# A four-layer graph network on one core: storing one running-maximum row per pair of steps, and a node tile's transform in one piece

## The chip, the cores and the metric

The kernel runs on one core of a Trainium2 chip. The metric is device time of one execution in microseconds (us); smaller is better. A core has a matrix engine (PE, with its weight loads shown as PEld), a vector engine (DVE), an activation engine (ACT), a general engine that also builds the descriptors of indirect transfers (POOL), and a queue engine (SP) that here only issues transfers. Every engine works through its own queue strictly in order and waits on semaphores for the others. Transfers run on 16 DMA engines.

## The reference, cut to what matters

6250 nodes of 256 features and 100000 edges, sorted by destination `dst`. `dst` is drawn as 6250 times a squared uniform number, so nodes of small number have many edges: block by block the mean number of edges per node falls from over a hundred to about eight.

```python
deg = segment_sum(ones, dst)
h = relu(layernorm(x))
h = h @ W1_self + (segment_sum(h[src], dst) / max(deg, 1)) @ W1_neigh + b1     # layer 1, mean
hp = relu(h @ W2_pool + b2_pool)
hmax = segment_max(hp[src], dst)                                               # layer 2, max
h = h @ W2_self + hmax @ W2_neigh + b2
h = ((segment_sum(h[src], dst) + h) / (deg + 1)) @ W3_neigh + b3               # layer 3
h = h @ W4_self + (segment_sum(h[src], dst) / max(deg, 1)) @ W4_neigh + b4     # layer 4, mean
out = x + h @ W_fc + b_fc
```

The hidden width is 512. All of it is float32; the kernel carries float32 through the matrix engine's bf16 path by three bf16 parts of a row.

## The kernel before, in words

Nodes lie in 49 tiles of 128. The weights are multiplied together ahead of the work, so that a layer's dense part is one product per tile. `fast_path` holds all that is spoken of here; `general_path` runs afterwards only if a flag in the tile `bad` says that the edges did not fit what the fast path assumes.

**Layer 1** (lines 780 to 866). Neighbour sums of the first 8 tiles (the hubs) are dense products with an edge-count matrix that is built from one-hot matrices (`build`, L309; `dense`, L433). Those of the other 41 tiles come from `sums` (L356): 474 steps, each an indirect gather of 128 edge rows (POOL, L376 `ring<-tab_h`) and three matmuls with a one-hot matrix (L394). When a tile's sums are complete its `done1` runs: the mean, two transposes (L825), a copy to SBUF (L827), a product with `Wb` (L834), then the rows of `hp` are written to `tab_p` (L838). The tile's own rows are handled apart in `own1` (L788): transposed by six matmuls (L794), copied, multiplied by `Wa` (L804), and the result plus a bias row is written to `tab_g`; `done1` reads that row block back (`grow2`, L819) and adds it. Both halves of the transposed rows also go to `tab_t`, which layer 2 reads. `own1` is advanced from inside `sums` by the iterator `beside`, so in program text all of it stands in the first 200 or so of the 474 steps.

**Layer 2** (lines 1008 to 1198). The 782 columns of edges are cut into six blocks of 52, 100, 200, 200, 130 and 100 columns (`BLOCKS`), worked from the last block to the first. Within a block of `tb` columns partition p holds `tb` consecutive edges. A step takes one column: an indirect gather of 128 rows of `tab_p` into half of a tile X (POOL, L1145), and one DVE instruction (L1150), X = max(previous X times `same`, X), in which `same` is 1 where the edge has the destination of the edge before it in the partition. So X is the running maximum of the run of equal destinations. After a pair of steps both rows of X, 512 KB, are stored to `runs[b]` (SP, L1181). There are six such X tiles in rotation. At a block's end `carry` joins runs over partitions (scan along the partitions, gather, maximum, scatter: L1023, L1035, L1041, L1042); its row number is `fixI`, from `segments`. Only then can `done2` of a node tile gather the row of each node's run end (L1054, at the row numbers `rows_of` from `node_rows`), transpose it, multiply (L1078, L1081, L1084), add (L1088), split into three parts and write `tab_r`. Beside this, `early_products` takes node tiles 37 to 6 in batches of four and multiplies them already for layer 3: per batch 16 results of 12 matmuls (L433 `pd<-r,ae`), each added by DVE to an accumulator (L942).

**Layers 3 and 4** have the shape of layer 1's `sums` with dense products for the first 16 and 18 tiles; the change does not touch them.

What sets the order: the Python text interleaves generators by step, but the order in which instructions stand in an engine's queue is made from it by a scheduler that works with its own estimate of each instruction. An instruction added in one place can move others on the same queue.

Of the kernel before, what the change touches and what calls it, by code (L numbers as in the profile page):

```python
# [25 lines left out]
G = 4  # L26
BLOCKS = (52, 100, 200, 200, 130, 100)
Z_SIGMA = 5.0
# [20 lines left out]
@with_exitstack  # L49
def kernel(ctx, tc, *aps):  # L50
    nc = tc.nc
    keep = ctx.enter_context(tc.tile_pool(name="keep", bufs=1))
    bad = keep.tile([P, 8], F32, name="bad")
    nc.vector.memset(bad, 0.0)
    fast_path(tc, bad, *aps)
    with tc.tile_pool(name="fl", bufs=1) as fp, tc.tile_pool(name="flp", bufs=1, space=PSUM) as pp:
        worst = fp.tile([P, 1], F32, name="worst")
        nc.vector.tensor_reduce(worst, bad, AX.X, ALU.max)
        ones = fp.tile([P, P], F32, name="ones_f")
        nc.vector.memset(ones, 1.0)  # L60
        pw = pp.tile([P, 1], F32, name="pw_f")
        nc.tensor.matmul(pw, ones, worst, start=True, stop=True)
        odd = fp.tile([P, 1], F32, name="odd")
        nc.vector.tensor_scalar(odd, pw, 1.0, None, op0=ALU.min)
        oddI = fp.tile([P, 1], I32, name="oddI")
        nc.vector.tensor_copy(oddI, odd)
        general = nc.values_load(oddI[:1, :1], min_val=0, max_val=1)
    with tc.If(general > 0):
        general_path(tc, *aps)
# [3 lines left out]
def fast_path(  # L73
# [82 lines left out]
    tab_p = dram.tile([NP, FH], F32, name="tab_p")  # L156
    tab_g = dram.tile([NP, FH], F32, name="tab_g")
    tab_r = dram.tile([NP, 3 * FH], BF16, name="tab_r")
    tab_s = dram.tile([NP, 3 * FO], BF16, name="tab_s")
    tab_a = dram.tile([H4, P, NT, P // 2], BF16, name="tab_a")  # L160
    xq = dram.tile([NP, FO], F32, name="xq")
    runs = [dram.tile([tb * P + 1, FH], F32, name=f"runb{b}") for b, tb in enumerate(BLOCKS)]
    dflat = dram.tile([EX + 32], I32, name="dflat")
# [5 lines left out]
    with tc.tile_pool(name="pads", bufs=1) as pp:  # L169
# [13 lines left out]
        nc.scalar.dma_start(sflat[E:EX].rearrange("(a b) -> a b", a=32), pads)  # L183
        for b, tb in enumerate(BLOCKS):
            nc.scalar.dma_start(runs[b][tb * P : tb * P + 1, :], zrow)

# [168 lines left out]

    def sums(pool, psg, table, F, srcT, keyT, jb, h, done, deep, hub, wait=0, counts=0, todo=(),  # L356
             beside=iter(())):

# [24 lines left out]
        for g in range(g_of[h][0], NG):  # L383
            pg = bank(psg, "pg", "pg", (F + counts,))
            n = min(G, T - g * G)
            for k in range(n):
# [13 lines left out]
                if at > wait:  # L400
                    hub.advance(math.ceil(len(hub.work) * (at - wait) / (T - j0 - wait)))
                next(beside, None)
                if todo and next(todo[0], None) is None:
# [47 lines left out]
    def scratch(n, dt=F32):  # L451

        t = xpool.tile([P, G2, FH], F32, name="X2").rearrange("p a b -> p (a b)")
        return (t if dt == F32 else t.bitcast(dt))[:, :n]

    def segments():
        dstI, dstF, eqf = scratch(T, I32), scratch(T), scratch(T)
        flen = ahead.tile([P, 1], F32, name="flenf")
        for b, tb in enumerate(BLOCKS):
# [11 lines left out]
        for b, tb in enumerate(BLOCKS):  # L471
# [7 lines left out]
            nc.vector.tensor_reduce(flen, eqf[:, sl_], AX.X, ALU.add)  # L479
            nc.vector.tensor_scalar(flen, flen, -1.0, float(P), op0=ALU.add, op1=ALU.mult)  # L480
            nc.vector.tensor_add(fixI[:, b : b + 1], flen, pidx)
            yield 1

# [293 lines left out]
    with ExitStack() as on:  # L777
# [9 lines left out]

        def own1(d):  # L788

            pt = bank(pst, "pt", "pt_h", (KI, P))  # L790
            for k in range(KI):
                for part in range(3):
                    c = part * FI + k * P
                    nc.tensor.matmul(pt[:, k, :], Z1[:, d, c : c + P], ident_b,  # L794
                                     start=(part == 0), stop=(part == 2))
            hT = wk.tile([P, KI, P], F32, name="h0T")
            nc.scalar.copy(hT, pt)
            nc.sync.dma_start(tab_t[d, :, : KI * P].rearrange("p (k n) -> p k n", n=P), hT)
            yield 1
            yield 1  # L800
            yield 1
            pm = bank(psm, "pm", "pm_g")
            for k in range(KI):
                nc.tensor.matmul(pm, hT[:, k, :], Wa[:, k, :], start=(k == 0),  # L804
                                 stop=(k == KI - 1))
            g = wk.tile([P, FH], F32, name="grow")
            nc.vector.tensor_add(g, pm, crow)
            nc.sync.dma_start(tab_g[d * P : (d + 1) * P, :], g)
            yield 1

        def done1(d, acc):
# [5 lines left out]
            nc.scalar.activation(m1, acc[:, :FI], AF.Copy, scale=r)  # L817
            g = wk.tile([P, FH], F32, name="grow2")
            nc.sync.dma_start(g, tab_g[d * P : (d + 1) * P, :])  # L819
            yield 1  # L820
            yield 1
            yield 1
            pt = bank(pst, "pt", "pt_m", (KI, P))
            for k in range(KI):
                nc.tensor.transpose(pt[:, k, :], m1[:, k * P : (k + 1) * P], ident)  # L825
            th = wk.tile([P, KI, P], F32, name="th")
            nc.scalar.copy(th, pt)  # L827
            nc.sync.dma_start(tab_t[d, :, KI * P :].rearrange("p (k n) -> p k n", n=P), th)
            yield 1
            yield 1  # L830
            yield 1
            ph = bank(psm, "pm", "pm_hp")
            for k in range(KI):
                nc.tensor.matmul(ph, th[:, k, :], Wb[:, k, :], start=(k == 0),  # L834
                                 stop=(k == KI - 1))
            nc.vector.tensor_add(g, ph, g)
            nc.scalar.activation(g, g, AF.Relu)
            nc.sync.dma_start(tab_p[d * P : (d + 1) * P, :], g)  # L838

# [13 lines left out]
        todo.append(segments())  # L853

        def owns():

            hubs = list(range(H1))
            for i, d in enumerate(range(H1, NT)):
                yield from own1(d)
                if i % 3 == 2 and hubs:  # L860
                    yield from own1(hubs.pop(0))
            for d in hubs:
                yield from own1(d)

        sums(wk, psg, tab_h, FI, srcT, keyT, JC * P, H1, done1, 14, hub, counts=1, todo=todo, beside=owns())
    layer1.close()


    def node_rows(pool, psm):
# [27 lines left out]
        for b, tb in enumerate(BLOCKS):  # L897
            z = float(tb * P)
            nc.vector.tensor_scalar(q, end, float(offs[b + 1]), -1.0 - offs[b], op0=ALU.min,
# [12 lines left out]
            nc.vector.tensor_add(pF, pF, off)  # L912
            nc.vector.scalar_tensor_tensor(t_, off, -float(tb), t_, op0=ALU.mult, op1=ALU.add)
            nc.vector.scalar_tensor_tensor(t_, t_, float(P), pF, op0=ALU.mult, op1=ALU.add)
            nc.vector.tensor_scalar(t_, t_, -z, None, op0=ALU.add)
# [31 lines left out]
    with tc.tile_pool(name="fl2c", bufs=1) as ck, ExitStack() as late:  # L947
# [188 lines left out]
        for b in reversed(range(NB)):  # L1136
# [3 lines left out]
            for s0 in range(0, tb, G2):  # L1140
                n = min(G2, tb - s0)
                X = (xmore if at // G2 % 2 else xpool).tile([P, G2, FH], F32, name="X2")
                for k in range(n):
# [34 lines left out]
                    for g in list(now):  # L1178
                        if next(g, 0) == 0:
                            now.remove(g)  # L1180
                nc.sync.dma_start(  # L1181
                    runs[b][s0 * P : (s0 + n) * P, :].rearrange("(g p) f -> p g f", p=P),
                    X[:, :n, :],
# [777 lines left out]
```

## Time and profile before

| what | us |
|---|---|
| runs | 3230.57, 3235.05, 3228.00; median 3230.57 |
| the profiled execution's own time | 3230.57 |
| its span | 3228.8 |
| layer 1, first gather to first gather of layer 2 | 147.75 to 855.0 |
| layer 2, first gather to last DVE step (L1150) | 855.0 to 2174.2 |
| layer 2, from there to the last gather of a run end (L1054) | 2174.2 to 2281.5 |
| layers 3 and 4 | to 3228.8 |

Counted along the gathers of L1145, layer 2's blocks begin at 855.0, 1006.0, 1222.3, 1546.1, 1879.3 and 2056.8 us: 1.51, 1.66, 1.62, 1.67, 1.78 and 2.24 us per step.

In the page's second part the span is cut into 40 slices of 80.7 us and each digit is a busy share in tenths. In a group of instructions the numbers after the bar are total busy time in us and the mean in ns of one, then the idle time of that engine just ahead of them and what ended it. In a list of waits each line gives who waited for whom, total us, times, and the longest. A table of stretches gives busy us and instruction count of each engine, then the granted PE clock, the DMA share and GB/s.

### The profile page before, as it was taken

Reading aid. Unit: us, or ns where it says so; the run is one execution under the profiler, and the core shown is the slowest. Engines: PE = TensorE matmul, PEld = TensorE weight load, DVE = VectorE, ACT = ScalarE, POOL = GpSimd, SP = SyncE. Lnnn points to the kernel's source line nnn. Section 1 sums busy time; section 2 is a strip of 40 time slices with the busy share of each in tenths; the row PEclk is TensorE's granted clock in tenths of the full one; section 3 lists DMA queues with packets and bytes.
Section 4 is the critical chain, followed back from the end, with each engine's and each line's share of the span. In section 5 each row is a group of like instructions: output and inputs, shape, how many; then the busy total and the mean of one; then the engine's idle time right before and its main releaser. Section 6 shows DMA issues by size and latency. Waiting matters only on the chain. (4 is left out here: it accounts for less than half of the span.)

```text
span 3228.8 us, 41603 instructions
## 1 busy us (share of the span) xinstructions
PE 2489.4 (77%) x12699; PEld 1410.8 (44%) x12699; DVE 1965.7 (61%) x5124; ACT 904.1 (28%) x2432; POOL 2032.8 (63%) x2260
## 2 busy tenths in 40 slices
PE   1468999888667566676677677679599999799997
PEld 1233666666433222233233233234234444488876
DVE  4854667665467676556556665553266767667665
ACT  2555667665245666211101110100000001000000
POOL 5272567777566766777666765550377767577764
PEclk9688999999889677888888888789899999899999
DMA  5454787777899999999999999991599999877774
GB/s 182 158 156 161 228 251 242 231 230 243 265 398 370 370 389 343 389 382 387 346 326 374 388 366 326 311 319 44 233 368 396 393 373 382 303 222 218 216 208 146
DMA packets 424577, 939.06 MB, mean 291 GB/s; under 512 B 60416, under 2 KB 166098, under 8 KB 424312
## 3 DMA queue, kind: packets, MB, share of 16 engines
q0 software_dynamic: 146560, 514.74, 47.1%
q1 hardware_dynamic: 219700, 366.14, 30.9%
q10 hardware_dynamic: 58084, 55.44, 5.3%
q8 instruction: 103, 1.69, 0.2%
q14 instruction: 130, 1.06, 0.1%
HBM read 623.50 MB, written 313.39 MB: 290 GB/s over the span
## 5 line engine op out<-in xcount | busy, mean ns | idle before, releaser
L1145 POOL DMA_INDIRECT X<-tab_p,srcIf x782 | 821.9, 1051 | 410.0 <-issue 185.4
L394 PE MATMUL pg<-ring,hot 128*128 128x256 bf16 (+2 forms) x3390 | 680.1, 310 | 114.0 <-DMA ring<-tab_h,srcT 63.7
L376 POOL DMA_INDIRECT ring<-tab_h,srcT x474 | 450.8, 951 | 239.4 <-PE pg L394 97.2
L433 PE MATMUL pd<-zt,ac 128*128 128x256 bf16 (+1 forms) x3462 | 571.4, 300 | 30.9 <-DMA ac<-tab_a 24.5
L433 PE MATMUL pd<-r,ae 128*128 128x512 bf16 x1536 | 407.0, 415 | 217.8 <-DVE acc L942 149.0
L394 PEld LDWEIGHTS <-hot 128*128 128x128 bf16 x3390 | 330.4, 99 | 343.7 <-issue 169.1
L1150 DVE SCALAR_TENSOR_TENSOR X<-X,samef,X 128x512 f32<-128x512 f32 x385 | 289.2, 751 | 278.9 <-DMA X<-tab_p,srcIf 191.4
L376 POOL DMA_INDIRECT ring<-tab_r,srcE x342 | 332.8, 973 | 150.2 <-PE pg L394 59.8
L433 PEld LDWEIGHTS <-ac 128*128 128x128 fp8e4 x3462 | 340.5, 99 | 165.6 <-issue 22.4
L1150 DVE SCALAR_TENSOR_TENSOR X<-X,samef 128x512 f32<-128x512 f32 x391 | 293.0, 750 | 172.5 <-DMA X<-tab_p,srcIf 168.1
L376 POOL DMA_INDIRECT ring<-tab_s,srcE x314 | 297.9, 949 | 129.0 <-PE pg L394 64.9
L433 PEld LDWEIGHTS <-ae 128*128 128x128 fp8e4 x1536 | 161.0, 105 | 473.1 <-issue 345.1
L309 PE MATMUL pb<-hm,hs 128*128 128x392 bf16 x781 | 257.4, 376 | 139.4 <-ACT A L313 63.1
L301 ACT ACTIVATE hs<-ht,onef 128x128 bf16<-128x128 bf16 x781 | 290.6, 395 | 232.0 <-PE pb L309 206.5
L414 DVE SCALAR_TENSOR_TENSOR acc<-pg,M,acc 128x257 f32<-128x257 f32 (+2 forms) x518 | 274.4, 561 | 79.5 <-PE pg L394 78.2
L1084 PE MATMUL pm_prf<-unf,hTf 128*128 128x512 f32 x392 | 203.1, 644 | 26.2 <-ACT hTf L1075 22.7
L1217 DVE TENSOR_SCALAR_CACHE_REDUCE many<-ac 128x896 bf16<-128x896 fp8e4 (+2 forms) x144 | 138.8, 964 | 129.5 <-DMA ac<-tab_a 129.5
L372 DVE TENSOR_SCALAR hot<-iota_bf,keyE 128x128 bf16<-128x128 bf16 x656 | 151.1, 273 | 67.5 <-PE pg L394 60.5
L303 DVE TENSOR_SCALAR hm<-iota_w,mk 128x392 bf16<-128x392 f16 x461 | 153.6, 339 | 60.0 <-PE pb L309 58.5
L313 ACT ACTIVATE A<-pb 128x392 fp8e4<-128x392 f32 x288 | 140.2, 491 | 170.8 <-PE pb L309 121.3
L433 PE MATMUL pd<-Z,A 128*128 128x256 bf16 (+1 forms) x1176 | 186.4, 273 | 0.4
L309 PEld LDWEIGHTS <-hs 128*128 128x128 bf16 x781 | 81.1, 104 | 225.1 <-issue 105.0
(275 smaller groups left out, 2819.1 us busy)
## 6 DMA issues: line engine op xcount, KB each, us to landing
runb<-X SPq DMA_DIRECT2D x391, 512.0 KB
tab_r<-r SPq DMA_DIRECT2D x49, 384.0 KB
tab_a<-A SPq DMA_DIRECT2D x18, 784.0 KB
tab_g<-grow SPq DMA_DIRECT2D x49, 256.0 KB
grow<-tab_g SPq DMA_DIRECT2D x49, 256.0 KB
tab_p<-grow SPq DMA_DIRECT2D x49, 256.0 KB
th<-tab_t ACTq DMA_DIRECT2D x49, 256.0 KB
X<-tab_p,srcIf POOLq DMA_INDIRECT x782
```

Of the source, the lines that this page charges most:

```text
L301: nc.scalar.activation(hots[0], t, AF.Relu, bias=one, scale=-1.0)
L303: nc.vector.tensor_scalar(hots[1], iota_w, mk[:, r : r + 1], None, op0=ALU.is_equal)
L309: nc.tensor.matmul(hold[0], hots[0], hots[1], start=(k == 0), stop=(k == k_of[w] - 1))
L313: nc.scalar.copy(A[:, :, c : c + WIN], hold[0].rearrange("p (s c) -> p s c", c=WIN), saturate=True)
L372: nc.vector.tensor_scalar(hot[j], iota_b, keyT[:, j - jb : j - jb + 1], None, op0=ALU.is_equal)
L376: nc.gpsimd.indirect_dma_start(out=ring[:, j % deep, : 3 * F], out_offset=None, in_=table, in_offset=bass.IndirectOffsetOnAxis(ap=srcT[:, ...
L394: nc.tensor.matmul(pg[:, : F + c], hot[j], X[:, part * F : (part + 1) * F + c], start=(k == 0 and part == 2), stop=(k == n - 1 and part == 1),
L414: nc.vector.scalar_tensor_tensor(acc[d], pg, m, acc[d], op0=ALU.mult, op1=ALU.add)
L433: nc.tensor.matmul(hold[0][:, : F + c], a, z[:, part * F : (part + 1) * F + c], start=(s == ss[0] and part == 2), stop=(s == ss[-1] and pa ...
L1084: nc.tensor.matmul(pm, hT[:, c, :], un[:, c, :], start=False, stop=(c == KH - 1))
L1145: nc.gpsimd.indirect_dma_start(out=X[:, k, :], out_offset=None, in_=tab_p, in_offset=bass.IndirectOffsetOnAxis(ap=srcI[:, t : t + 1], axis=0),
L1150: nc.vector.scalar_tensor_tensor(X[:, k, :], prev, same[:, t : t + 1], X[:, k, :], op0=ALU.mult, op1=ALU.max,)
```

## The change

Layer 2. For blocks 0, 1 and 2 (`MERGED = 3`) a pair of steps stores one row instead of two. After the pair's two steps one more DVE instruction forms, in the tile's first row, max(second row times `same` of the second step, first row): the second row where the second edge goes on with the run of the first, else the first row, which is then a run's end. Only that row, 256 KB, is stored; the last pair of a block still stores both. `runs[b]` has `tb // 2 + 1` row groups in these blocks; row numbers in `segments` and `node_rows` are converted by `kept_row`. A run that lies wholly in the second step of a pair would be lost, so `bad` gets three more columns that flag it. The cut between blocks 2 and 3 moves from 200 and 200 columns to 220 and 180.

Layer 1. `own1`, `owns`, `tab_g` and `beside` go. `done1` does the six own transposes and the two of the mean into one bank, copies them at once, writes them to `tab_t` with one transfer, and accumulates the products with `Wa` and `Wb` in one bank, to which the bias row is added. It has three yields where it had six.

```diff
-BLOCKS = (52, 100, 200, 200, 130, 100)
+BLOCKS = (52, 100, 220, 180, 130, 100)
+MERGED = 3
...
+    kept = [tb // 2 + 1 if b < MERGED else tb for b, tb in enumerate(BLOCKS)]
+    runs = [dram.tile([n * P + 1, FH], F32, name=f"runb{b}") for b, n in enumerate(kept)]
...
-                next(beside, None)
...
+    def kept_row(b, t, whole, half):
+        nc.vector.tensor_copy(whole, t)
+        nc.vector.tensor_single_scalar(whole, whole, 1, op=ALU.logical_shift_right)
+        nc.vector.tensor_copy(half, whole)
+        nc.vector.tensor_scalar(t, t, -(BLOCKS[b] / 2.0 - 1.0), None, op0=ALU.add)
+        nc.vector.tensor_tensor(t, t, half, op=ALU.max)
...
+            if b < MERGED:
+                two = eqf[:, t0 : t0 + tb // 2 - 1]
+                nc.vector.tensor_tensor(two, same[:, t0 + 1 : t0 + tb - 2 : 2],
+                                        same[:, t0 + 2 : t0 + tb - 1 : 2], op=ALU.add)
+                nc.vector.tensor_scalar(two, two, 0.0, None, op0=ALU.is_equal)
+                nc.vector.tensor_reduce(bad[:, 8 + b : 9 + b], two, AX.X, ALU.max)
...
         def done1(d, acc):
...
-            g = wk.tile([P, FH], F32, name="grow2")
-            nc.sync.dma_start(g, tab_g[d * P : (d + 1) * P, :])
             yield 1
-            yield 1
-            yield 1
-            pt = bank(pst, "pt", "pt_m", (KI, P))
+            pt = bank(pst, "pt", "pt_m", (2 * KI, P))
             for k in range(KI):
-                nc.tensor.transpose(pt[:, k, :], m1[:, k * P : (k + 1) * P], ident)
+                for part in range(3):
+                    c = part * FI + k * P
+                    nc.tensor.matmul(pt[:, k, :], Z1[:, d, c : c + P], ident_b,
+                                     start=(part == 0), stop=(part == 2))
+            for k in range(KI):
+                nc.tensor.transpose(pt[:, KI + k, :], m1[:, k * P : (k + 1) * P], ident)
...
+            nc.sync.dma_start(tab_t[d].rearrange("p (k n) -> p k n", n=P), th)
             yield 1
             ph = bank(psm, "pm", "pm_hp")
             for k in range(KI):
+                nc.tensor.matmul(ph, th[:, k, :], Wa[:, k, :], start=(k == 0), stop=False)
+            yield 1
+            for k in range(KI):
+                nc.tensor.matmul(ph, th[:, KI + k, :], Wb[:, k, :], start=False,
                                  stop=(k == KI - 1))
...
+                r0 = s0
+                if b < MERGED:
+                    r0 = s0 // 2
+                    if s0 + n < tb:
+                        t = t0 + s0 + 1
+                        nc.vector.scalar_tensor_tensor(
+                            X[:, 0, :], prev, same[:, t : t + 1], X[:, 0, :],
+                            op0=ALU.mult, op1=ALU.max,
+                        )
+                        n = 1
                 nc.sync.dma_start(
-                    runs[b][s0 * P : (s0 + n) * P, :].rearrange("(g p) f -> p g f", p=P),
+                    runs[b][r0 * P : (r0 + n) * P, :].rearrange("(g p) f -> p g f", p=P),
                     X[:, :n, :],
                 )
```

## The prediction

> **What bounds the kernel now.** I read the page's slices first, then a table of stretches cut where the work changes, then the groups and waits inside each. From the slices:
>
> ```profile
> PE   1468999888667566676677677679599999799997
> DVE  4854667665467676556556665553266767667665
> ...
> POOL 5272567777566766777666765550377767577764
> ...
> DMA  5454787777899999999999999991599999877774
> ```
>
> DMA stands at 9 through all of layer 2 (slices 12 to 27, counted from 1) but for one hole, slice 28: DMA 1, POOL 0, PE 9. The stretches say what the hole is:
>
> ```profile
> core 0: us, PE busy (x) PEld busy (x) DVE busy (x) ACT busy (x) POOL busy (x), PEclk, DMA share, GB/s
> 270.00:500.00 230.00, 226.66 (x1359) 140.02 (x1358) 133.67 (x410) 130.35 (x362) 125.12 (x132) 1.00 0.76 237
> 500.00:853.00 353.00, 308.26 (x2148) 219.94 (x2146) 210.38 (x787) 217.50 (x585) 251.02 (x264) 0.99 0.76 234
> 855.00:1546.00 691.00, 453.55 (x1374) 211.48 (x1375) 443.19 (x948) 295.72 (x838) 487.49 (x461) 0.80 1.01 377
> 1546.00:2175.00 629.00, 434.34 (x1451) 189.69 (x1451) 371.58 (x580) 74.73 (x159) 398.07 (x384) 0.84 0.97 344
> 2175.00:2282.00 107.00, 100.94 (x384) 46.82 (x382) 34.94 (x68) 9.11 (x15) 6.51 (x7) 0.98 0.19 60
> ```
>
> Five regimes. 270 to 500, layer 1 with the own transforms in it: PE is busy 226.66 of 230, the bound. 500 to 853, layer 1 after them: POOL, whose issues take 951 ns and follow one another after 0.30 us, so 1.25 us a gather; 264 of them fill 330 of the 353 us. 855 to 1546, blocks 5 to 3: DMA at share 1.01. 1546 to 2175, blocks 2 to 0: still DMA at 0.97, with DVE 59% busy. 2175 to 2282: PE alone, with nothing else to do. The groups of the first, second, fourth and fifth stretch that carry the sums below:
>
> ```profile
> L804 PE MATMUL pm_g<-Wa,h0T 128*128 128x512 f32 x196 | 94.8, 606 | 3.0 <-ACT h0T L797 1.2 <-DVE grow L807 0.6
> ...
> L794 PE MATMUL pt_h<-ident_b,Z 128*128 128x128 bf16 x288 | 24.7, 219 | 0.1
> L834 PE MATMUL pm_hp<-Wb,th 128*128 128x512 f32 x48 | 22.8, 597 | 0.0
> ```
>
> ```profile
> L834 PE MATMUL pm_hp<-Wb,th 128*128 128x512 f32 x148 | 70.9, 598 | 3.5 <-DVE grow L836 3.5
> ```
>
> ```profile
> L1145 POOL DMA_INDIRECT X<-tab_p,srcIf x352 | 365.4, 1038 | 196.7 <-issue 73.4 <-DVE X L1150 56.2 <-DMA runb<-X 37.0
> L433 PE MATMUL pd<-r,ae 128*128 128x512 bf16 x953 | 264.2, 426 | 167.7 <-DVE acc L942 139.1 <-DVE r L279 27.3 <-DMA runb<-X 1.2
> ...
> L1150 DVE SCALAR_TENSOR_TENSOR X<-X,samef,X 128x512 f32<-128x512 f32 x175 | 131.4, 751 | 142.0 <-DMA X<-tab_p,srcIf 88.9 <-issue 44.5 <-DVE X L1150 3.5
> ...
> L942 DVE TENSOR_TENSOR acc<-acc,pd 128x512 f32<-128x512 f32 x81 | 55.2, 681 | 2.8 <-PE pd L433 2.8
> ```
>
> ```profile
> L433 PE MATMUL pd<-r,ae 128*128 128x512 bf16 x260 | 60.1, 384 | 0.0
> ```
>
> ```profile
> POOL runb L1042 <- DVE fixf L1041: 101.1, 2, 90.2
> ```
>
> The reader is to see a queue effect. While gathers run, PE is not the limit: it waits 139.1 us for DVE's additions, because those stand behind steps that wait for gathered rows. Then the last step is done and 260 early products are still to come, with 23 additions behind them; the last carries wait behind them too (the last line: the scatter of a carry waits 90.2 us). That is work late in the queues, not work that had to be late.
>
> **The change, part by part.** Span 3228.8, the execution 3230.57 (1.8 outside the span), which is also the median shown; so the sum is made against 3230.57.
>
> *The extra maximum.* 183 of the 186 pairs of blocks 2 to 0 issue one more L1150-like instruction at 0.751: +137 us of DVE. Counted in the order of the changed build's DVE queue, from the start of block 2 to the last step: 369 + 183 of these (414.6 us), 104 additions of early products at 0.681 (70.8), 28 tiles' three instructions at 0.687 (57.7), 15 further additions (10.3), 37 one-hot rows at 0.338 (12.5), scans and small ones (20): 586 us. Before, DVE had 371.6 us of work in the 629 us.
>
> *The halved stores.* 183 stores lose 0.262 MB each, 48 MB. What the 372 steps then move: gathers 97.5, stores 49.5, the tiles' run ends, `tab_t` and `tab_r` 27, `tab_a` 7: 181 MB, at the 377 GB/s that a full DMA reached here 480 us. POOL: 372 issues of 1.038 + 0.30, 33 run ends and some fixes, 550 us. So the bound of these blocks passes from DMA to DVE (586), with POOL close behind. The trace shows no stretch with DVE as bound. Lower end: DVE without a gap, 586. Upper end: the pace of block 0 now, 2.24 us a step, 834. I take 641, DVE busy 91%, because other bounds here reach 87 to 94%: POOL 330 of 353 in layer 1, POOL 626 of 691 (487.5 plus 0.30 for each of 461) beside the full DMA. Against it stands what the same 372 steps take now: 629 plus 20 steps of block 3 at 1.62, 661. Gain 20.
>
> The Trainium skill, "GPSIMD Engine Reference", section Specifications, speaks against the change: POOL's SBUF interface is shared with DVE and contends with DVE instructions that have two SBUF inputs, as the new maximum has. The rows agree in direction (issues of 951 ns in layer 1, where DVE's large operations read PSUM, and 1038 here). If all of that rise came from this cause it would grow with DVE's share of such instructions, from 42% of the time to 65%, to some 1.09 us, an estimate from that page's rule, and POOL would need 569 instead of 550; the sum would not change, since 586 stays above.
>
> *The early products.* In the changed build's DVE queue no addition of an early product stands behind the last step; the 23 of before are all spread among the steps, as are the instructions of five of the six tiles that came last. What is left behind the last step is the last carry and tile 0. Its price from the rows at the end of the old stretch: scans begin 2270.39, maximum 2275.62, scatter 2276.57, last run end gathered 2281.52, so 11 us, with some 6 us for the last store to land and the fix rows to be gathered behind it. 107 becomes 17 to 25: gain 88 at 19. Both ends: 92, or 50 if a PE that lags still holds up transposes. That this work now lies among the steps is already in the 586. PE's share there: 434 + 85 moved + 20 for the shifted steps, 539 of 641 at the clock of 0.84; it stays below.
>
> The same place has a second rule: "TensorE: Matmul & The Clock Gate", What's actually happening, says that PE's clock is halved after an idle window and restored by sustained work. Row: granted clock 0.98 in the dense stretch, 0.84 among the steps, 384 against 426 ns a product. By the rule alone the 260 moved products could take up to twice their time, 60 us more of PE; by the rows 11. Neither makes PE the bound.
>
> *Own transform into `done1`.* One own transform costs PE 2.1 us: their starts lie 2.83 apart (273.56 and 276.39) with 0.7 us of step matmuls between. From 270 to 500 that is 49 x 2.1 = 103 of the 227 busy us. They go; 12 tiles' `done1` run in this stretch (x48 in the row, four to a tile) and get 2.1 each, 25. PE then needs 149, and POOL's 132 gathers at 1.25 us are 165: the bound becomes POOL, gain 65. From 500 on 37 tiles (x148) bring 78 us to a PE that is busy 308 of 353: 386, over POOL's 330, so PE becomes the bound there; with 3% of waits 398, loss 45. Net gain 20. Ends: PE never idle would be 535 of 583, gain 48; if each of the 49 tiles makes PE wait the 0.37 to 0.6 us of the copy, because one step now separates transposes and product where three did, the gain is gone and 10 are lost. The tail of layer 1 (831.35 to 855) loses a wait of 4.05 us for the reload of `tab_g` and gets 2.1 of PE: nothing.
>
> *Edits at nothing.* 25.7 MB through `tab_g`, in and out: DMA share 0.76, hidden; if it were not, 25.7 MB at 235 GB/s would be a gain of 109, which the trace excludes by its two other bounds. SP issues two transfers a tile in place of five; nobody waits for SP in layer 1. One addition of 0.69 us less per tile, off the bound (DVE 58 to 60% busy). Some 33 small instructions in `segments` and 15 in `node_rows`, 0.15 to 0.25 us each, 9 us: beside a DVE that is 58% and 64% busy; without that cover, -9. The cut at 220: tile 11 becomes ready with block 2, its `done2` moves some 45 steps, and the batch it belongs to forms one step later: nothing.
>
> Sum: 20 + 20 + 88 = 128, so 3102.
>
> **The rivals.** *A: DVE without gaps.* Blocks 2 to 0 in 590 to 600 (gain 65) and layer 1 at 40: 3230 - 65 - 40 - 90 = 3035 to 3070. For it: DVE waits just 2.8 us for PE in these blocks now. Against: no engine here is above 94% while DMA is not the bound. *B: the hole is not removed but spread.* PE, POOL and DVE all near 85 to 90% hold each other up, blocks 2 to 0 take 690 to 740, layer 1 gives nothing: 3175 to 3225 at the far end, 3150 at the near. For it: blocks 1 and 0 already run at 1.78 and 2.24 a step, where several tiles' work comes at once. *C: slower.* The one place is the DVE queue of blocks 2 to 0: an addition that waits for PE stops the steps behind it, the six X tiles fill, POOL stops. It decides from 661 + 88 + 20 = 769 us for 372 steps, 2.07 a step, DVE below 76%. For it: the pace of block 0; against it: DMA is at 75% there and DVE's waits now are for DMA. *D: the change doesn't do what it says:* a run of one edge in the second step of a pair would set the flag, and the general path would run all four layers once more behind this one. At block 2's end a node has about 17 edges; I leave it at less than 1%.
>
> **How the numbers follow.** Likeliest 60% (3070 to 3145), A 15%, B 15%, C 8%, no change that can be told 2%. Something within 0.2%, 6.5 us, can't be told from no change here. So faster 0.90, same 0.02, slower 0.08. The range leaves out C and the ends of A and B: 3045 to 3185.
>
> **What would show it.** Right: no stretch of PE alone after the last step, last run end gathered 15 to 25 us after it; DVE at 88% or more in blocks 2 to 0 and DMA at 0.8 or less; gathers of layer 1 at 1.25 us from 275 on, then PE at 97% or more to the end of layer 1, layer 2's first gather near 835. Wrong: DVE idle on PE in blocks 2 to 0; waits of PE for the copy `th` in layer 1; layers 3 and 4, 3228.8 - 2281.5 = 947 us after the last run end, of another length.

## The result, and the profile after

The changed kernel takes 3086.72 us (median of 4 runs, 3084.84 to 3090.12), the kernel before beside it 3229.28 (4 runs): ratio 0.9558, 95% interval 0.9541 to 0.9574. That is 142.6 us less, where 128 were forecast (3102). The profiled execution took 3087.14 with a span of 3085.3. By stages, in us of the profiled executions:

| stage | before | after | forecast | measured |
|---|---|---|---|---|
| to the first gather of layer 2 | 855.0 | 821.0 | -20 | -34.0 |
| layer 2, the first 410 steps | 660.9 | 664.8 | 0 | +3.9 |
| layer 2, the last 372 steps | 658.3 | 625.0 | -20 | -33.3 |
| from the last step to the last run end's gather | 107.4 | 12.3 | -88 | -95.1 |
| layer 3, to its last gather | 483.1 | 495.2 | 0 | +12.1 |
| the rest | 464.2 | 467.1 | 0 | +2.9 |

The slices of the page after; the hole that was slice 28 is gone from POOL and DMA:

```profile
PE   1568999999768555666789997972899899799997
DVE  4955666655367677555789997974466667576665
...
POOL 5274777776366776777667777764676677677663
...
DMA  5454667776599999999989998976999999777774
```

The stretches after, cut at the same places in the work. The columns are length, then busy us and instructions of PE, PEld, DVE, ACT and POOL, then the granted clock of PE, the DMA share and GB/s:

```profile
270.00:500.00 230.00, 215.78 (x1445) 146.64 (x1444) 142.81 (x524) 157.03 (x433) 170.91 (x180) 1.00 0.67 201
500.00:821.00 321.00, 311.20 (x2042) 209.60 (x2039) 167.71 (x622) 176.04 (x450) 204.91 (x217) 1.00 0.66 199
821.00:1485.00 664.00, 436.11 (x1316) 203.91 (x1317) 427.27 (x935) 291.70 (x830) 462.73 (x441) 0.80 1.01 374
1485.00:2111.00 626.00, 512.79 (x1877) 231.21 (x1877) 538.49 (x847) 87.31 (x182) 448.41 (x408) 0.92 0.90 297
2111.00:2125.00 14.00, 7.55 (x16) 3.42 (x15) 2.87 (x11) 0.00 (x0) 3.86 (x4) 0.74 0.29 96
```

In layer 1 the gathers now run ahead (180 from 270 to 500 where there were 132), and PE is the bound from 500 on, 311.20 of 321 us. In the fourth stretch DMA has gone from share 0.97 at 344 GB/s to 0.90 at 297. DVE is busy 538.49 of 626 us (86%). POOL is busy 448.41, and with the 0.30 us that follow each of its 408 instructions it needs 571, 91%; in what follows this sum is called POOL's need. The groups of that stretch:

```profile
L1137 POOL DMA_INDIRECT X<-tab_p,srcIf x373 | 411.3, 1103 | 147.1 <-issue 81.4 <-DVE X L1142 26.8 <-DMA runb<-X 14.2
L435 PE MATMUL pd<-r,ae 128*128 128x512 bf16 x1248 | 305.9, 393 | 52.5 <-DVE acc L934 43.6 <-DVE r L283 8.8
...
L1178 DVE SCALAR_TENSOR_TENSOR X<-X,samef 128x512 f32<-128x512 f32 x183 | 137.1, 750 | 4.0
```

All 183 extra maxima are there at 750 ns and hardly wait (4.0 us in all). A gather's issue takes 1103 ns where it took 1038. And behind the last step there is nothing but the last carry and tile 0. Their four POOL instructions, each with its start, its length and what it waited for:

```profile
2114.35 0.94 POOL L1027 DMA_INDIRECT fixf<-runb,fixIf  x1 [7.70 <-DMA runb<-X]
2118.72 1.00 POOL L1034 DMA_INDIRECT runb<-fixf,fixIf  x1 [3.43 <-DVE fixf L1033]
2121.74 0.97 POOL L1046 DMA_INDIRECT tot<-runb,rows_of  x1 [2.02 <-DMA runb<-fixf,fixIf]
2123.01 0.95 POOL L1046 DMA_INDIRECT tot<-runb,rows_of  x1 [0.30 <-issue]
```

### The profile page after: what moved, and what is told of

It reads as the page before. It is cut to its first block, busy times and chain, and to the rows that moved or that the text cites. A ratio compares the mean times of both kernels' runs of the same rounds, so it can differ in the third digit from the quotient of the medians.

```text
span 3085.3 us, 41397 instructions
## 1 busy us (share of the span) xinstructions
PE 2456.4 (80%) x12699; PEld 1401.4 (45%) x12699; DVE 2053.6 (67%) x5303; ACT 893.7 (29%) x2383; POOL 2054.0 (67%) x2260
## 5 line engine op out<-in xcount | busy, mean ns | idle before, releaser
L1137 POOL DMA_INDIRECT X<-tab_p,srcIf x782 | 842.3, 1077 | 368.6 <-issue 170.5
L435 PE MATMUL pd<-r,ae 128*128 128x512 bf16 x1536 | 383.4, 399 | 102.9 <-DVE acc L934 46.9
```

Source lines behind the costliest of these rows:

```text
L435: nc.tensor.matmul(hold[0][:, : F + c], a, z[:, part * F : (part + 1) * F + c], start=(s == ss[0] and part == 2), stop=(s == ss[-1] and pa ...
L1137: nc.gpsimd.indirect_dma_start(out=X[:, k, :], out_offset=None, in_=tab_p, in_offset=bass.IndirectOffsetOnAxis(ap=srcI[:, t : t + 1], axis=0),
```

## The experiments

The theory to be tested is the prediction's own: four causes that add up (order in DVE's queue, halved stores, the extra maximum's price, a lighter early layer 1). The rivals: that the halved transfers carry all of layer 2's gain, or that the extra instruction costs nothing. The stage times below are cut as in the table above.

### Each part of the change alone

`e1` has layer 1 of after and layer 2 of before:

```diff
-BLOCKS = (52, 100, 220, 180, 130, 100)
-MERGED = 3
+BLOCKS = (52, 100, 200, 200, 130, 100)
+MERGED = 0
```

> Only the own transform is moved into done1; layer 2 stays as before. If the two parts of the change are independent, layer 2 begins near 821 instead of 855, as it did in the changed kernel, the stretch of PE alone at the end of layer 2 stays near 107 us, and the time is 3229 - 34 = 3195 (3188 to 3202). If the 12 us that layer 3 lost in the changed kernel come with this part (no tab_g, another layout of the tables), 3207. If layer 1's gain needs the other part, 3225 or more.

3205.0 us, ratio 0.9948 (0.9930 to 0.9966). Layer 2 starts at 822.4, 33 us earlier, and the tail is as before, 108.8. Against the kernel before beside it (3220.9) 16 of the 33 us are left at the end. Layer 3 is 9 us longer here too (492.3); that is taken up below. The other 8 can't be placed: this kernel before is 8 us faster than the one beside the result, and no trace of it was taken here.

`e2` has layer 2 of after, with `own1`, `tab_g`, `beside` and `done1` as before.

> Only layer 2's part; layer 1 as before (first gather of layer 2 at 855). Independent parts: tail 107 to 12, blocks 2 to 0 in 625 where 661 were due, block 3 6 us longer: 3229 - 95 - 36 + 6 = 3104, and 3116 if layer 3's 12 us belong to this part. If the tail or the pace needs layer 1's part too, above 3130.

3107.32 us, ratio 0.9647 (0.9607 to 0.9686). Layer 2 starts at 856.2, its last 372 steps take 622.5, its tail 12.4. The product of the two ratios is 0.9597, that of the whole 0.9558; the 0.4% between them is half the width of `e2`'s interval, so no larger effect of the parts on each other is seen.

### What the layer 2 part is made of

`e3` is `e2` with the extra maximum kept but both rows stored, as before (the diff is cut: the sizes of `runs[b]` and the row numbers are those for two rows too):

```diff
-                    r0 = s0 // 2
...
-                        n = 1
```

> As the run with layer 2's part alone, but both rows of a pair are stored, at the row numbers of before: the extra maximum without the saved bytes. My theory, the place of the early products in the queues makes the stretch of PE alone: no addition stands behind the last step in this build, so the tail is 12 to 20 us; blocks 2 to 0 are bound by DMA again (229 MB at 377 GB/s, 608 us, with PE, DVE and POOL beside it) and take 640 to 670 for 372 steps; 3130 to 3150. Rival, the saved bytes are what gives the gain and the extra maximum is only a cost: tail 60 or more, blocks 2 to 0 above 670, 3220 or slower than before.

`e4` is `e2` with half the rows stored but without the extra maximum. It leaves that maximum out, so what it stores is not always a run's end, and the maxima of some nodes lack edges:

```diff
-                        t = t0 + s0 + 1
-                        nc.vector.scalar_tensor_tensor(
-                            X[:, 0, :], prev, same[:, t : t + 1], X[:, 0, :],
-                            op0=ALU.mult, op1=ALU.max,
-                        )
```

> As the run with layer 2's part alone, but without the extra maximum: one row of a pair is stored as it is, so the maxima of some nodes lack edges. The saved bytes without the DVE work. My theory: 27 additions stand behind the last step in this build, so the stretch of PE alone stays, 100 to 115 us; blocks 2 to 0 lose their DMA bound without getting DVE work and go to POOL's pace, 590 to 620 for 372 steps; 3165 to 3195. Rival, the bytes give the gain: tail gone, 3080 to 3110.

`e3`: 3140.53 us, ratio 0.9760 (0.9712 to 0.9809); `e4`: 3196.79, ratio 0.9917 (0.9889 to 0.9944). The kernel that adds work and saves no transfer gains far more than the one that saves the transfer and adds nothing. Their stages say why. `e3` (the profiled execution took 3127.41, the fastest of its four) has 656.4 us in the last 372 steps, no better than before, and a tail of 12.4; `e4` has 591.2 there and a tail of 124.7. These are the last two stretches of `e3`, then of `e4`:

```profile
1512.00:2168.00 656.00, 528.18 (x1856) 236.32 (x1889) 540.91 (x847) 87.50 (x182) 440.88 (x407) 0.90 0.99 356
2168.00:2181.00 13.00, 7.99 (x16) 3.74 (x16) 3.23 (x12) 0.00 (x0) 3.11 (x4) 0.63 0.28 103
```

```profile
1526.00:2117.00 591.00, 429.30 (x1410) 187.49 (x1436) 383.67 (x597) 76.68 (x164) 417.58 (x403) 0.85 0.91 303
2117.00:2242.00 125.00, 118.73 (x449) 54.87 (x456) 40.47 (x77) 10.93 (x18) 7.27 (x8) 0.99 0.17 57
```

In `e4` the hole is back, 118.73 us of PE alone. The tail goes with the extra maximum, not with the stores. But the maximum itself does nothing for the early products. The likely reason is that it makes a pair of steps longer in the scheduler's estimate, and so the scheduler places the early products' additions among the steps; the estimates themselves were not recorded. What the traces show is the order. In DVE's queue 23 additions of early products stand behind the last step in the kernel before, 27 in `e4`, and none in `e2`, `e3` or after.

`e7` tests this directly. It is the kernel before, with no instruction added or removed; only an order is asked for: the next step's maximum is to stand behind the newest early addition in DVE's queue.

```diff
+    added = [None]
...
-            nc.vector.tensor_add(acc3[d], acc3[d], v)
+            added[0] = nc.vector.tensor_add(acc3[d], acc3[d], v)
...
-                        nc.vector.scalar_tensor_tensor(
+                        step = nc.vector.scalar_tensor_tensor(
...
+                        if added[0] is not None:
+                            tc.add_manual_dep(
+                                getattr(step, "ins", step), getattr(added[0], "ins", added[0]).name,
+                                mybir.DependencyInfo(mybir.DependencyClass.NoSync,
+                                                     mybir.DependencyReason.DATA),
+                                reason="order")
+                            added[0] = None
```

> The kernel before with nothing added or taken away but an order on DVE's queue: the next step of the running maximum may not be placed ahead of the last addition of an early product that the program text puts before it. No addition stands behind the last step in this build. Theory (the stretch of PE alone is a matter of queue order): tail 107 to 12, the 372 last steps 658 to 640-675 as with the extra maximum and full stores (656), 3130 to 3150. Rival (the longer DVE work or the saved bytes are needed to make room for the products among the steps): the steps stretch by what the tail gives, 740 or more, 3210 to 3230.

`e9` is `e4` with the same order asked for (without the extra maximum too, so the maxima of some nodes lack edges here as well).

> One row of a pair stored and no extra maximum (the maxima of some nodes lack edges), with the same order edges on DVE's queue. Beside the run with layer 2's part alone (622 for the 372 steps, tail 12, 3107) it differs by the 137 us of DVE work alone. If DVE's work bounds these steps, they fall to 590 or less and the time to 3075 or less; if POOL's pace bounds them (373 issues of 1.10 + 0.30 and 41 others, 570 to 580) they take 605 to 625, 3090 to 3110.

`e7`: 3123.52 us, ratio 0.9688 (0.9662 to 0.9713). Order alone is worth 103 us, nearly three quarters of the whole change. `e9`: 3103.8, ratio 0.9630 (0.9600 to 0.9660). The last 372 steps and the tail of `e7`, then of `e9`:

```profile
1530.00:2163.00 633.00, 483.18 (x1706) 218.01 (x1738) 408.95 (x641) 76.97 (x160) 422.31 (x407) 0.88 1.00 366
2163.00:2175.00 12.00, 7.53 (x16) 3.48 (x16) 2.87 (x11) 0.00 (x0) 2.91 (x3) 0.70 0.27 101
```

```profile
1534.00:2130.00 596.00, 469.62 (x1706) 214.10 (x1737) 410.36 (x644) 77.20 (x160) 427.01 (x407) 0.89 0.92 308
2130.00:2142.00 12.00, 7.74 (x16) 3.61 (x16) 2.87 (x11) 0.00 (x0) 2.92 (x3) 0.69 0.25 87
```

Now four kernels form a square, all with the tail gone. The one not shown yet is `e2`; its last 372 steps are:

```profile
1520.00:2142.00 622.00, 511.25 (x1849) 231.78 (x1881) 537.61 (x846) 87.35 (x182) 442.34 (x407) 0.92 0.90 298
```

The numbers are the last 372 steps in us, and in brackets POOL's need as a share of the stretch:

| | both rows stored | one row stored |
|---|---|---|
| no extra maximum | `e7` 632.6 (86%) | `e9` 595.6 (92%) |
| extra maximum | `e3` 656.4 (86%) | `e2` 622.5 (91%) |

Down the columns the maximum costs 24 and 27 us; along the rows the halved stores give 37 and 34. Not all of that is the maximum or the stores: in `e7` and `e9` the order asked for moves 9 and 8 of the 106 early additions to ahead of these steps, and the 410 steps before take 18 and 15 us longer than in `e3` and `e2`. Over all 782 steps the maximum costs 6 and 12 us, and the halved stores give 34 and 28.

With both rows DMA is full (share 0.99 and 1.00), and 82 to 83% of POOL's instructions start within 0.35 us of the end of the one before. With one row DMA is at 0.90 to 0.92 and 92% of POOL's instructions do (94% after), so POOL issues nearly without a break: as far as the traces tell it is the bound, with DMA close behind (0.92 as well in `e9`). A POOL at 90% would not prove that alone: from 821 to 1485 us after, beside a DMA share of 1.01, its need is 90% too. `e9` shows that DVE is not the bound: its DVE has a third of its time to spare (69% busy, 86% in `e2`), and yet POOL stands at 92%. Its 595.6 us lie between the 590 or less that was expected for DVE as the bound and the 605 to 625 for POOL.

So the extra maximum's price doesn't come from filling DVE. It shows in POOL's issues. Here are the groups of gathers in the last 372 steps of `e7`, `e9`, `e3` and `e2`, in this order:

```profile
L1146 POOL DMA_INDIRECT X<-tab_p,srcIf x372 | 386.5, 1039 | 185.7 <-issue 77.3 <-DVE X L1151 64.5 <-DMA runb<-X 17.3
```

```profile
L1172 POOL DMA_INDIRECT X<-tab_p,srcIf x372 | 389.8, 1048 | 151.9 <-issue 71.9 <-DVE X L1177 46.5 <-DMA runb<-X 13.7
```

```profile
L1167 POOL DMA_INDIRECT X<-tab_p,srcIf x372 | 403.0, 1083 | 188.2 <-issue 76.7 <-DVE X L1172 46.5 <-DMA runb<-X 20.7
```

```profile
L1171 POOL DMA_INDIRECT X<-tab_p,srcIf x372 | 404.9, 1089 | 147.8 <-issue 78.3 <-DVE X L1176 30.4 <-DMA runb<-X 13.9
```

1039 and 1048 ns without the maximum, 1083 and 1089 with it, whatever is stored. 41 to 44 ns on 372 issues are 15 to 16 us, the size of that price. The trace after shows it inside one run, too: of POOL's 406 indirect issues in the last 372 steps, the 42 during which DVE runs no maximum take 964 ns on average, and the 212 with more than 0.8 us of maxima beside them take 1137. (A long issue also has more time for maxima beside it; the 42 don't depend on that.)

### How the two parts could be better

`e5` is the kernel before with the own transforms of layer 1 spread over twice the steps, and nothing else:

```diff
-                next(beside, None)
+                if (j - j0) % 2 == 0:
+                    next(beside, None)
```

> The kernel before with own1 advanced at every second step, so that the 49 own transforms stand over nearly all of layer 1's 474 steps; tab_g and its reload stay. Theory (layer 1's gain is the even load of PE): layer 2 begins at 820 to 830, 3222 - 28 = 3190 to 3200. Rival (the gain is the dropped reload, add and transfers): 845 or more, 3215 or more.

3176.39 us, ratio 0.9838 (0.9817 to 0.9859), layer 2 starts at 809.0 against 821.0 after. That is more than the theory expected. So layer 1's gain doesn't need the work or the traffic that the one-piece form saves (`tab_g` is still written and read here): it is enough to spread the own transforms. PE, which was busy 308.26 of 353 us from 500 on before, is now full to the end:

```profile
270.00:500.00 230.00, 227.86 (x1486) 152.66 (x1485) 148.32 (x518) 155.74 (x448) 159.72 (x168) 0.99 0.81 252
500.00:809.00 309.00, 296.79 (x2021) 208.43 (x2018) 188.34 (x683) 184.29 (x500) 217.29 (x230) 0.99 0.82 257
```

The form after is 12 us later because PE has more left to do behind the last gather: 31.7 us from 782 to 821, about 10 of them own transforms of the last tiles and the rest products still due, against 14.1 in `e5`. After, the last gather of layer 1 is issued at 782.4 and the first of layer 2 comes 38.6 us later, when the last rows of `tab_p` are there; in `e5` it is 785.8 and 23 us. The wait, from the list after:

```profile
POOL X L1137 <- DMA tab_p<-hpf: 37.7, 1, 37.7
```

`e6` is the changed kernel with `MERGED = 4`, that is with block 3 merged too:

> The changed kernel with MERGED = 4: block 3 too stores one row for a pair (90 more maxima, 24 MB less). If saved bytes outweigh DVE work where DMA is full (share 1.01, DVE 64% busy), block 3 goes from 1.65 to 1.50-1.58 a step, 3065 to 3075. If DVE or POOL already bound it, no change within 0.3% of the changed kernel, 3080 to 3095.

3062.63 us, ratio 0.9481 (0.9458 to 0.9505): 24 us better than the change as made, and the best time of all kernels here. But it did not come where it was expected: block 3 takes 1.63 us a step where the change has 1.65 and 1.50 to 1.58 were expected, and POOL's need in the first 410 steps rises from 90 to 93%. The gain lies in the last 372 steps, 607.0 us for 625.0, of whose 106 early additions 11 now stand among the steps before.

### Layer 3, and other chips

Layer 3 takes 483 to 484 us in the kernels whose tables in DRAM have their old sizes and order (before, `e5`, `e7`) and 487 to 495 in all the others (487.2 in `e3`, whose `runs` have the old size in all but another cut between blocks 2 and 3). `e13` tests whether the place of the later tables matters: it is the changed kernel with `tab_g` allocated again, unused, and a further tensor that fills what the smaller `runs` leave.

```diff
+    tab_g = dram.tile([NP, FH], F32, name="tab_g")
...
+    fill = dram.tile([(T - sum(kept)) * P, FH], F32, name="fill")
```

> The changed kernel with the DRAM tables at the places of before: a tab_g that nothing reads and one filler of the size that runb lost, each touched by one 2 KB write. Layer 3, from the last run end gathered to the last gather of tab_r, took 483.1, 483.2 and 484.4 us in three kernels with the old places, 487 to 492 in three with smaller runb or without tab_g, 494 to 495 in three others, and its instructions are the same. If the places of the tables are the cause, 483 to 486 here and 3075 for the whole; if not, 490 to 496 and the changed kernel's time.

`a1` is the changed kernel once more, on the same chip, to compare with:

> The changed kernel once more, beside the run with the old places of the tables: 3078 to 3090, layer 3 493 to 497, first gather of layer 2 at 821, tail 12.

These ran on another chip, on which the kernel before takes 3456.09 us. `e13`: 3453.65, ratio 0.9994 (0.9978 to 1.0011); `a1`: 3450.87, ratio 0.9993 (0.9978 to 1.0008). Layer 3 takes 530.2 us with the old places and 528.3 with the new: they give nothing back there. On the first kind of chip it wasn't tried, and where the 12 us come from stays open.

The greater finding is that on this chip the change gains nothing. The tail is gone here too (12.4 us), but layer 1 lasts to 1049.2 us where it lasted to 821.0. `e14` is `e2` with `MERGED = 4` and the own transforms at half pace, as in `e5`:

> What the runs so far point to as the fastest: layer 2's part with MERGED = 4, and layer 1 not as changed but as before with own1 at every second step. If the parts add up: first gather of layer 2 at 809 in place of 822, the rest as in the run with MERGED = 4 (3061): 3045 to 3055. If half-paced own transforms lose their gain beside the other queue order, 3060 to 3095.

3340.17 us on this chip, ratio 0.9683 (0.9627 to 0.9739), layer 2 starts at 956; the forecast was for the first kind of chip, where this kernel was not run. So the layer 2 part gains here too, and the form of layer 1 seems to decide. The last run is `e2` once more:

> The layer 2 part alone once more (layer 1 as before). On a chip where the kernel before takes 3220 to 3230 us every theory expects the first result again, 3107 (ratio 0.965), with layer 1 to 856 us. The run is for a chip where before takes about 3456 and the whole change gained nothing (3451, layer 1 to 1049). Theory 'on such a chip the denser TensorE work of the new layer 1 loses what layer 2 gains': this kernel starts layer 2 near 940 to 960 and takes 3330 to 3350 (ratio 0.964 to 0.97), the tail still 12 us. Rival 'the whole chip is slower in layer 1 whatever its form, and the tail of before is short there': layer 2 starts near 1050 and the time is 3440 to 3460 (ratio 0.996 to 1.0).

It fell on another chip of the same kind (before 3454.84): 3362.85 us, ratio 0.9727 (0.9680 to 0.9774). Layer 2 starts at 966.7, the tail is 12.4. The first theory's numbers are met nearly (start 940 to 960, ratio 0.964 to 0.97), the rival's (1050, 0.996) not at all. Across these two chips the new layer 1 costs 1049.2 - 966.7 = 82.5 us, where it gains 34 on the first kind; the totals of `a1` and `e15` lie 88 apart. The traces show what happens. First layer 1 of `a1` in stretches, then that of `e15`:

```profile
270.00:500.00 230.00, 168.66 (x915) 101.47 (x915) 101.96 (x357) 123.80 (x353) 111.52 (x117) 0.81 0.44 131
500.00:821.00 321.00, 252.98 (x1451) 161.95 (x1450) 142.93 (x504) 160.45 (x417) 165.37 (x175) 0.85 0.49 147
821.00:1049.00 228.00, 193.24 (x1177) 125.21 (x1174) 88.66 (x324) 85.09 (x204) 99.71 (x105) 0.95 0.49 150
```

```profile
270.00:500.00 230.00, 212.37 (x1184) 122.27 (x1184) 120.81 (x378) 133.31 (x388) 102.57 (x108) 0.93 0.65 203
500.00:821.00 321.00, 260.04 (x1625) 174.05 (x1622) 168.85 (x622) 185.92 (x506) 200.23 (x211) 0.91 0.65 194
```

On the first kind of chip the granted clock was 1.00 in both stretches of after. Here it is 0.81 and 0.85 with the new layer 1 and 0.93 and 0.91 with the old one, and PE often stands still: between 270 us and the last gather of layer 1 there are 46 pauses of more than 1 us in `a1`, 137 us in all, 25 in `e15` with 61 us, and 3 with 4 us in the changed kernel on the first kind of chip. Part of the timeline of PE in `a1`, a tile's product after pauses and the next tile's without one:

```profile
618.43 0.44 PE L824 MATMUL pt_m<-identf,m 128*128 128x128 f32 x2 [3.21 <-ACT m L815]
...
622.61 3.52 PE L831 MATMUL pm_hp<-Wa,th 128*128 128x512 f32 x4 [2.18 <-ACT th L826]
...
631.86 1.98 PE L831 MATMUL pm_hp<-Wa,th 128*128 128x512 f32 x4 [0.37 <-issue]
```

The same four matmuls take 3.52 us and then 1.98. The granted clock (the third number from the end) is half of the full one from just after the pause of 3.21 us to 625.73, and full around the second product:

```profile
618.91:625.73 6.82, 4.64 (x12) 2.10 (x11) 1.10 (x6) 1.86 (x4) 2.48 (x3) 0.50 0.53 154
631.80:634.00 2.20, 2.15 (x7) 1.07 (x8) 0.54 (x3) 1.19 (x4) 0.95 (x1) 1.00 0.80 238
```

This group has a mean of 836 ns from 270 to 950 us in `a1` and 612 in layer 1 of the changed kernel on the first kind of chip:

```profile
L831 PE MATMUL pm_hp<-Wa,th 128*128 128x512 f32 x188 | 131.1, 836 | 45.5 <-ACT th L826 31.0 <-issue 11.1 <-ACT hs L305 3.3
```

```profile
L831 PE MATMUL pm_hp<-Wa,th 128*128 128x512 f32 x193 | 94.6, 612 | 2.6 <-ACT th L826 2.1
```

The Trainium skill, "TensorE: Matmul & The Clock Gate", What's actually happening, says that PE runs at half its clock after an idle window, of about 3.4 us, and until it has been busy for one. These rows agree: 1.78 times as long at a clock of 0.50, granted behind a pause of 3.21 us.

Of the 137 us of pauses in `a1`, 57 us in 14 of them are waits for a tile's row mean (ACT, L815) and 30 in 12 for the copy `th` (ACT, L826). The one-piece form leaves one step where three stood, both between the row mean and PE's transposes and between the copy and the product, so a late ACT stops PE sooner; that this is how the form loses is argued from these waits, not shown by a run. What starts the pauses on such chips is not shown: some waits of ACT and DVE (one of 18 us by ACT at 158 us) end with nothing that the trace records. No trace of the kernel before was taken on such a chip.

## Why the prediction was right, and where it was not

**The early products: right.** 88 forecast, 95.1 measured. No stretch of PE alone was left, and the last run end was gathered 12.3 us after the last step, where 17 to 25 were said; the last store's landing and the fix rows, for which 6 us were set aside, ran beside the scans within the 11. That it is a matter of queue order was the prediction's reading of the trace; `e7` shows it without any other change. The rule on the halved clock would have made the moved products up to twice as long; measured, a product takes 393 ns in the stretch at a clock of 0.92, less than the 426 of before at 0.84. It was right not to price it.

**Blocks 2 to 0: the gain too small, the bound named wrongly.** 641 forecast for the 372 steps, 625.0 measured. The step that failed is "DVE (586)" as the new bound. DVE's union is 538 us for the same instructions, because two neighbours overlap when the second waits for nothing. In the timeline of after an instruction of 0.75 us is followed by the next 0.66 later:

```profile
2108.40 0.75 DVE L1178 SCALAR_TENSOR_TENSOR X<-X,samef 128x512 f32<-128x512 f32 x1
2109.06 0.75 DVE L1142 SCALAR_TENSOR_TENSOR X<-X,samef,X 128x512 f32<-128x512 f32 x1
```

The sum of durations, which is 586 in the trace as well, is thus 9% above what DVE needed. The Trainium skill says this, in "Perfetto Trace Analysis", Optimizing Scalar/DVE Operations: half of the data-access overhead that a profile shows for an instruction overlaps with the next one. POOL was the bound instead, with 571 us where the rows had given 550. The forecast's 91% of a bound came true for another engine than the one it was made for, 571 of 626 us; that is luck.

The signs "DVE at 88% or more" and "DMA at 0.8 or less" failed too: DVE is at 86%, and the DMA share is 0.90. The bytes were nearly right (181 MB forecast, 297 GB/s over 626 us are 186). But 480 us of DMA time for them were reckoned at 377 GB/s, and the measured share stands for 563 us, at 330 GB/s. So DMA stayed close to being the bound.

**POOL's issues: the page was nearer than the rows.** The prediction weighed a rule of "GPSIMD Engine Reference", Specifications (POOL's SBUF interface contends with DVE instructions that have two SBUF inputs) and estimated 1.09 us an issue from it, against 1.038 by the row. Measured: 1.103 after, 1.083 and 1.089 in `e3` and `e2`, and 1.039 to 1.048 without the maximum. POOL's need, 569 by that rule, measured 571. The rule was set aside because DVE's 586 stood above it; with 538 it did not. The runs show the longer issues beside the maxima; that the shared interface is their cause is the page's rule.

**Layer 1: right in kind, too small in size.** 20 forecast, 34.0 measured. Cut at 437 us after, where as many gathers are done as at 500 before (from the stretches of after):

```profile
270.00:437.00 167.00, 154.87 (x1035) 104.69 (x1033) 103.03 (x378) 113.27 (x314) 123.13 (x130) 1.00 0.67 200
437.00:821.00 384.00, 372.11 (x2452) 251.55 (x2449) 207.49 (x766) 219.81 (x568) 252.69 (x267) 1.00 0.66 200
```

The early part takes 167 us where 165 were forecast (-63 for -65). The late part takes 384 where 398 were: +31 for +45. The term that was mis-sized is PE's need there, "386", which measured 372; the 3% of waits on top of it were right. The tail of layer 1, priced at nothing, is part of the late part: it grew from 23.7 to 38.6 us, while the gathers ended 49 us earlier. Layer 2 starts at 821, not "near 835".

**Layers 3 and 4: wrong.** "Of another length" they are, 962.3 us instead of 947. The prediction had no term for them, and the cause was not found.

**The rivals.** *A* (DVE without gaps, 3035 to 3070) is refuted for this change: DVE is at 86%. *B* (the hole spread over the steps) is seen in small: in `e7` the first 410 steps take 14.6 us more than before, from work that moved in among them. *C* (DVE's queue holds the steps up) did not come: in the last 372 steps DVE waits 1.6 us in all for PE, at 106 additions. *D* did not happen.

**The sum: closer than its terms.** Against the forecast the three gains together came out 34 us larger, and three stages priced at nothing lost 19; that the two partly cancel is luck.

What the prediction did not see is that the sign of layer 1's part depends on the chip. It had named the wait for the copy as the way to lose the gain there (10 us lost at the low end). On the first kind of chip PE waits 2.1 us for it from 270 to 821 us; on the other kind this wait and the one for the row mean are most of the pauses.

## What to carry to other kernels

When one engine works alone behind the end of a phase, look first at which instructions stand late in which queue: here an order-only dependency took 95 of 107 us of such a tail away, and 103 us off the whole, without any change of work; the halved stores gave about 30. Price an engine's need by the union of its busy time, not by a sum of durations, and look for the bound again after every step: easing DMA uncovered POOL, whose issues lengthened with the added DVE work. A test with one cause changed at a time was needed, since on one chip the kernel that only added work gained 80 us and the one that only saved transfers 24.

## What the runs showed of the hardware that was not expected

- The time depends on the chip: the kernel before takes 3221 to 3229 us on some and 3455 to 3456 on two others. Between the changed kernel's traces on the two kinds the granted clock of PE differs in layer 1 (1.00 against 0.87 from 270 us to its end) and by 0.01 or less in the later layers. A change that packs PE more tightly gains 34 us on the one kind and loses about 82 on the other.
- An indirect gather's issue on POOL takes 951 ns on average in layer 1, where DVE runs no running maximum, 1039 to 1048 beside one maximum a step, and 1083 to 1103 beside half as many again; within one run, 964 with no maximum beside it and 1137 with more than 0.8 us.
- In the last 372 steps POOL's need was 82 to 86% of the time at a DMA share of 0.97 to 1.00 and 91 to 92% at 0.90 to 0.92. A full DMA alone does not set that: in the steps before it was 90% at 1.01.
